# Graph convolution, first layer: each gather waits for a unit of the product, and the next layer's weights are loaded in the fourth group

## The chip, the cores and the metric

One core of a Trainium2 chip. The metric is the device time of one execution in microseconds (us); the median of ten executions of the kernel before is 502.68 us (502.14 to 503.23). Engines: PE (TensorE; its weight loads are listed as PEld), DVE (VectorE), ACT (ScalarE), POOL (GpSimd) and SP (SyncE, which here only issues DMAs).

## The reference

A layer norm and a relu, then three layers of edge convolution over 80,000 edges between 2,500 nodes of 256 features, then one product over the four concatenated stages, added to x. The edges come sorted by target.

```python
def _edge_conv(x, src, dst, W, b):
    xi = x[dst]
    xj = x[src]
    m = jnp.concatenate([xi, xj - xi], axis=-1) @ W + b
    s = jax.ops.segment_sum(m, dst, num_segments=N)
    cnt = jax.ops.segment_sum(jnp.ones((dst.shape[0],), m.dtype), dst, num_segments=N)
    return s / jnp.maximum(cnt, 1.0)[:, None]
...
for W, b in ((W0, b0), (W1, b1), (W2, b2)):
    h = jax.nn.relu(_edge_conv(h, src, dst, W, b))
    xs.append(h)
cat = jnp.concatenate(xs, axis=-1)
return cat @ Wf + bf
...
h = jnp.maximum(_layernorm(x, axis=-1), 0.0)
x = x + _L0_gnn_ref(h, edge_index, ...)
```

## The kernel before

`by_windows` turns the segment sum into a product. `a` holds, for a group of targets, how many edges go from each of 2,560 padded nodes to each target. A layer first forms z, the nodes times the lower half of W, split in two parts `zh` and `zl` whose sum is z. It then forms z times `a`, to which it adds the nodes times the upper half.

**Groups and units.** Targets 112 to 2,499 stand in five groups (`NG`) of at most 480. `layer` (L989) computes one group as a generator: 20 units of four matmuls (two halves of the features, `zh` and `zl`, for one tile of 128 nodes) and four units with the weights `wt`. In the first layer the counts of the next group are made between the units (`build`, `finish`). In the first layer, the matmuls of all five groups, 120 units, run from 61 to 198 us. The loop over the groups of the first layer (from L1079) also steps a generator `extra` once or twice a unit; it holds the small works that are to be spread out: the degrees of the nodes (`degrees`), `later_loads`, and `shares` in the last group.

**The first 112 targets** (`FEW`) aren't in the groups. For them z is gathered edge by edge: z of the first layer is stored to `z_dram[0]` (`keep_nodes`: `zh` from SP's queue, `zl` added to it from POOL's), and `gather(0)` (L918) issues 56 gathers (`EDGES`) from POOL, one for the e-th edge of every target, each of 128 rows of 1 KB. `who` gives the rows; where a target has no e-th edge it points at one fixed row of padding (`NONE`, L618). The gathers go to the eight places of `sums` in turn, from the ninth on adding to what is there. `add_sums` (L926) adds `b_all` times the degree, then adds the eight places up on DVE and splits the result in two parts; `layer_few` (L977) takes it into PSUM with two matmuls against `only` for each half of the features, after the ones with `wt`.

**Order.** An engine called through `InOrder` (PEo, DVEo, POOLo, ACTo, SPo) keeps the order in which the program was written; what is called without it is placed by a scheduler. On PE `layer_few(0)` stands after the last unit of the first layer and before `nodes_split` (L784), the first step of layer 1. In layers 1 and 2 the gathers are made by `gather_pairs` (L954), without adding, and from the fifth pair on the first of each pair waits for the latest matmul unit issued in the program.

**Loads and stores on SP.** `later_loads` (L1065) loads layer 1's weights (`wb`, `wt`, `wf`), the bias rows `b_all` of layer 0 and `bf_sb`. `store_a` writes the counts of the first four groups to DRAM when they are complete, four stores each, for layers 1 and 2.

Of the kernel before, what the change touches and what calls it, by code (L numbers as in the profile page):

```python
# [11 lines left out]
OP = mybir.AluOpType  # L12
# [295 lines left out]
def chain(*its):  # L308
    for it in its:
        yield from it  # L310
# [3 lines left out]
def by_windows(ctx: ExitStack, tc: tile.TileContext, x, src, dst, Ws, bs, Wf, bf, out, missing):  # L314
    nc = tc.nc
    PE, DVE, ACT, POOL, SP = nc.tensor, nc.vector, nc.scalar, nc.gpsimd, nc.sync
    PEo, DVEo, POOLo, ACTo, SPo = (InOrder(tc, e) for e in (PE, DVE, POOL, ACT, SP))
# [3 lines left out]
    NT = (N + P - 1) // P  # L321
# [3 lines left out]
    DC = D // P  # L325
# [7 lines left out]
    EDGES = 56  # L333
    SUMS = 8
# [3 lines left out]
    WG = (NW + P - 1) // P  # L338
# [36 lines left out]
    def bank():  # L375
        return ps[-1].tile([P, 512], F32, name="bank")
# [42 lines left out]
    def tile_of(z, t):  # L419
        return z[:, t % 2, t // 2 * D:(t // 2 + 1) * D]  # L420
# [23 lines left out]
    def load_wb(l, queue=SP):  # L444
        ws[l] = wpool.tile([P, DC, D], F32, name="wt"), wpool.tile([P, DC, D], F32, name="wb", bufs=1)
        queue.dma_start(ws[l][1], Ws[l][D:2 * D, :].rearrange("(c p) d -> p c d", p=P))

    def load_wt(l, queue=SP):
        queue.dma_start(ws[l][0], Ws[l][0:D, :].rearrange("(c p) d -> p c d", p=P))
# [205 lines left out]
    def degrees(i):  # L655

        for q in range(W + 2):
            junk = hot.tile([P, CAP], BF16, name="junk2")
            ACTo.activation(junk, away[:, i, :], AF.Relu, bias=nc_[:, q:q + 1], accum_out=gsum[:, i, q:q + 1])
            yield  # L660
        DVEo.scalar_tensor_tensor(deg[:, i, :], gsum[:, i, 1:W + 1], -2.0, gsum[:, i, 0:W], op0=OP.mult, op1=OP.add)
        DVEo.tensor_add(deg[:, i, :], deg[:, i, :], gsum[:, i, 2:W + 2])
        DVEo.tensor_copy(deg_b[:, i, :], deg[:, i, :])
        yield
        yield
        yield
        yield
        for w0 in range(0, min(P, NW - i * P), P // 2):
            n = min(P // 2, NW - i * P - w0)
            pc = bank()  # L670
            for c in range(W):
                PEo.matmul(pc[:, :n * W].rearrange("p (w c) -> p w c", c=W)[:, :, c],
                          deg_b[:, i, c:c + 1].to_broadcast([P, P]), ident_b[:, w0:w0 + n], start=True, stop=True)
            to = FEW + (i * P + w0) * W
            ACTo.copy(cnt[:, to:to + n * W], pc[:, :n * W])
            yield
        if i == WG - 1:
            pc = bank()
            PEo.matmul(pc[:, :FEW], deg_b[:, i, 0:1].to_broadcast([P, P]), ident_b[:, IN_LAST:IN_LAST + FEW],
                       start=True, stop=True)  # L680
            ACTo.copy(cnt[:, :FEW], pc[:, :FEW])
            yield
# [136 lines left out]
    def group_of(g):  # L819
        return FEW + sum(GWS[:g]) * W, GWS[g] * W  # L820
# [5 lines left out]
    def new_a(g):  # L826
        return apools[g % 2].tile([P, NT, GS], F32R, name="a")
# [50 lines left out]
    def finish(g, a):  # L878
        c0, n = group_of(g)
        if n < GS:  # L880
            DVEo.memset(a[:, :, n:].bitcast(F32), 0.0)
        ACTo.copy(a[PAD:PAD + 1, NT - 1, :n], cnt[PAD:PAD + 1, c0:c0 + n])
        if g + 1 < NG:
            store_a(g, a)
        yield

    def store_a(g, a, queue=SP):

        for t in range(0, NT, 5):
            queue.dma_start(a_dram[g][:, t:t + 5, :], a[:, t:t + 5, :].bitcast(F32))  # L890
# [13 lines left out]
    def keep_nodes(l, a, b):  # L904
# [4 lines left out]
        def tiles_of(z):  # L909
            return z[:, :, a // 2 * D:b // 2 * D].bitcast(F32).rearrange("p i (q d) -> p i q d", d=D)  # L910
# [4 lines left out]
        for i, q in ways:  # L915
            POOLo.dma_start(to[:, i, q, :], tiles_of(zl)[:, i, q, :], accum_op=OP.add)

    def gather(l):  # L918

        for e in range(EDGES):  # L920
            POOLo.indirect_dma_start(
                out=sums[:, e % SUMS, :], out_offset=None, in_=z_dram[l][:, :],
                in_offset=bass.IndirectOffsetOnAxis(ap=who[:, e:e + 1], axis=0),
                **({"compute_op": OP.add} if e >= SUMS else {}))

    def add_sums(n):  # L926

# [9 lines left out]
    def room(as_=F32):  # L937

        return hot.tile([P, BW * CH, P], BF16, name="one_m", bufs=AHEAD).rearrange(
            "p k m -> p (k m)").bitcast(as_).rearrange("p (i d) -> p i d", i=2)  # L940
# [13 lines left out]
    def gather_pairs(l):  # L954

        got = []
        for k in range(EDGES // 2 + PAIRS):
            if k >= PAIRS:
                if k == PAIRS + 1:
                    DVEo.tensor_add(sums[:, :2, :], got[0], got[1])  # L960
                elif k > PAIRS:
                    DVEo.tensor_add(sums[:, :2, :], sums[:, :2, :], got[k - PAIRS])
            if k < EDGES // 2:
                two = room()
                got.append(two)
                for i in range(2):
                    d = POOLo.indirect_dma_start(
                        out=two[:, i, :], out_offset=None, in_=z_dram[l][:, :],
                        in_offset=bass.IndirectOffsetOnAxis(ap=who[:, 2 * k + i:2 * k + i + 1], axis=0))
                    if k >= PAIRS and i == 0:  # L970

                        tc.add_manual_dep(d.ins, unit[0].ins.name, mybir.DependencyInfo(
                            mybir.DependencyClass.Sync, mybir.DependencyReason.DATA), reason="spread over the layer")
            if k >= PAIRS - 1:
                yield

# [10 lines left out]
    unit = [None]  # L987

    def layer(l, g, a, own, PE=PE, ACT=ACT):  # L989

        c0, n = group_of(g)
        pa = ps_agg.tile([P, DC, 512], F32, name="pa")
        ways = [(o, c) for o in range(DC) for c in range(DC)]
        units = [(0, k) for k in BY_TURNS]
        for i, u in enumerate(own):
            units.insert(u + i, (1, i))
        last = {}
        for kind, i in units:
            last.update({o: (kind, i, o) for o in (range(DC) if kind == 0 else ways[i][:1])})
        for kind, i in units:  # L1000
            if kind == 0:
                for o in range(DC):
                    for z in (zh, zl):
                        unit[0] = PE.matmul(pa[:, o, :n], tile_of(z, i)[:, o * P:(o + 1) * P], a[:, i, :n],  # L1004
                                            start=(i == 0 and z is zh),
                                            stop=(z is zl and last[o] == (kind, i, o)))
            else:
                o, c = ways[i]
                unit[0] = PE.matmul(pa[:, o, :n], ws[l][0][:, c, o * P:(o + 1) * P], hT[:, c, c0:c0 + n],  # L1009
                                    start=False, stop=(last[o] == (kind, i, o)))  # L1010
            yield
        ACT.activation(hT[:, :, c0:c0 + n], pa[:, :, :n], AF.Relu)  # L1012
# [8 lines left out]
    a = new_a(0)  # L1021
# [43 lines left out]
    def later_loads():  # L1065
        load_wb(1, SPo)
        load_wt(1, SPo)
        load_wf(1, SPo)
        load_b_all(0, SPo)
        SPo.dma_start(bf_sb, bass.AP(tensor=bf.tensor, offset=bf.offset, ap=[[0, P], [1, D]]))  # L1070
        yield
# [2 lines left out]

    held = None
    LATE = [NT] * 4
    gather(0)
    extra = chain(degrees(0), finish(0, a), later_loads(), degrees(1))
    for g in range(NG):  # L1079
        at = {}  # L1080
        own = LATE
        if g + 1 < NG:
            a1 = new_a(g + 1)
            one = build(g + 1, a1)
            left = -(-len([b for b in windows if b[0] == g + 1]) // TURN)
            units = NT + DC * DC
            at = {(i + 1) * (units - 1) // left - 1 for i in range(left)}
            if g:
                own = [u + 1 - i for i, u in enumerate(sorted(at)[1:5])]
        else:  # L1090
            extra = shares()
        for u, _ in enumerate(layer(0, g, a, own, PEo, ACTo)):
            if u in at:
                next(one)
            next(extra, None)
            if g == 0 and u % 2:
                next(extra, None)
            if g == 0 and u == NT // 2 + 3:
                by_count(0)
            if u == NT - 1 and g + 1 < NG:  # L1100
                run(extra)
                by_count(g + 1)
                if g == NG - 2:
                    by_count(NG)
        run(extra)
        if g + 1 < NG:
            run(finish(g + 1, a1))
            held, a = a, a1
        extra = chain(degrees(g + 2) if g + 2 < WG else ())
    layer_few(0, add_sums(SUMS))  # L1110
    DVEo.tensor_sub(ws[1][0], ws[1][0], ws[1][1])
    tiles = {NG - 1: a, NG - 2: held}
# [81 lines left out]
```

## Time and profile before

| | |
|---|---|
| median of 10 executions | 502.68 us |
| the profiled execution | 502.23 us |
| its span | 500.4 us |
| granted PE clock | 0.998 |
| first layer's last unit ends on PE | about 198.4 us |
| first gather starts | 76.34 us |
| last gather starts | 184.52 us |
| gathers of the first layer (`sums<-z_dram,who`) | 56, mean 1660 ns on POOL |
| loads of `later_loads` issued by SP | 76.12 to 80.2 us |
| stores of `a`, groups 1 to 3, issued by SP | 91.35 to 152.0 us, 12 of 1200 KB |

All times in a profile are counted from the start of the span. A line of a timeline gives the start, the length, the engine, the line of code, the operation, what it writes and reads, and in brackets how long the engine was idle before it and what ended that idle time. Operations of the ordered engines all stand under L282, the line of the helper. In the table by stretch the columns are: the stretch, its length, busy time and instructions of PE, PEld, DVE, ACT and POOL, the granted PE clock, the mean busy share of the 16 DMA engines, and GB/s. A DMA queue's line gives its packets, its MB and the time of its packets as a share of 16 engines' stretch; q0 is POOL's queue, q1 SP's. "DMA to landing" is the time from the start of the issuing instruction to the last byte's arrival.

### The profile page before, as it was taken

Reading aid. Unit: us, or ns where it says so; the run is one execution under the profiler, and the core shown is the slowest. Engines: PE = TensorE matmul, PEld = TensorE weight load, DVE = VectorE, ACT = ScalarE, POOL = GpSimd, SP = SyncE. Lnnn points to the kernel's source line nnn. Section 1 sums busy time; section 2 is a strip of 40 time slices with the busy share of each in tenths; the row PEclk is TensorE's granted clock in tenths of the full one; section 3 lists DMA queues with packets and bytes.
Section 4 is the critical chain, followed back from the end, with each engine's and each line's share of the span. In section 5 each row is a group of like instructions: output and inputs, shape, how many; then the busy total and the mean of one; then the engine's idle time right before and its main releaser. Section 6 shows DMA issues by size and latency. Waiting matters only on the chain.

```text
span 500.4 us, 7649 instructions
## 1 busy us (share of the span) xinstructions
PE 490.5 (98%) x2863; PEld 403.1 (81%) x2863; DVE 265.7 (53%) x670; ACT 135.1 (27%) x309; POOL 251.7 (50%) x234
## 2 busy tenths in 40 slices
PE   8999999999999999999999999999999999999994
PEld 4888888778788887888788787878887878778783
DVE  7999988888998802771243131427623231214043
ACT  5676577655634311510000000005200000000000
POOL 3688307888888870025777482600276545451000
PEclk9999999999999999999999999999999999999999
DMA  9416998796969994477999999963338699998032
GB/s 278 152 52 130 245 294 250 286 225 177 325 104 362 117 79 47 159 266 308 348 282 347 212 278 247 93 116 126 106 105 331 231 300 218 263 240 84 2 117 94
DMA packets 42104, 100.01 MB, mean 200 GB/s; under 512 B 5209, under 2 KB 32170, under 8 KB 36394
## 3 DMA queue, kind: packets, MB, share of 16 engines
q1 hardware_dynamic: 22762, 70.06, 38.5%
q0 software_dynamic: 18368, 28.26, 35.7%
q10 hardware_dynamic: 928, 1.11, 0.7%
q8 instruction: 24, 0.39, 0.3%
q14 instruction: 22, 0.18, 0.1%
HBM read 61.79 MB, written 38.26 MB: 200 GB/s over the span
## 4 chain that ended last, share of the span: by engine, by line
PE 91%; DVE 4%; DMA 2%; POOL 1%; SPq 0%; issue 0%; ACT 0%; DVEq 0%; ACTq 0%
PE pa L1004 34%; PE pa L282 22%; PE bank L811 10%; PE bank L282 7%; PE bank L787 7%; PE pa L1009 6%; PE pz L282 3%; DMA acc<-in_x_dram 2%; DVE one_m L282 1%; DVE st L282 1%; DVE one_n L282 1%; POOL acc L282 1%; DVE zl L282 0%; DVE away L282 0%; SPq L282 0%; PE turned L282 0%
## 5 line engine op out<-in xcount | busy, mean ns | idle before, releaser
L282 POOL DMA_INDIRECT one_m<-z_dram,who x112 | 110.6, 988 | 145.8 <-DVE acc L282 70.9
L1004 PE MATMUL pa<-a,zh 128*128 128x480 f32 (+1 forms) x400 | 151.8, 379 | 0.0
L1004 PE MATMUL pa<-a,zl 128*128 128x480 f32 (+1 forms) x400 | 151.7, 379 | 0.0
L282 POOL DMA_INDIRECT sums<-z_dram,who x56 | 93.0, 1660 | 25.4 <-issue 16.8
L282 DVE TENSOR_TENSOR sums<-sums,one_m 128x512 f32<-128x512 f32 x52 | 36.1, 693 | 105.9 <-DMA one_m<-z_dram,who 105.5
L1004 PEld LDWEIGHTS pa<-a,zl 128*128 128x128 f32 x400 | 75.0, 187 | 12.1
L1004 PEld LDWEIGHTS pa<-a,zh 128*128 128x128 f32 x400 | 75.1, 188 | 10.3
L282 PE MATMUL pa<-a,zh 128*128 128x480 f32 (+1 forms) x200 | 81.1, 406 | 0.0
L282 PE MATMUL pa<-a,zl 128*128 128x480 f32 (+1 forms) x200 | 75.7, 379 | 0.0
L282 DVE TENSOR_TENSOR one_m<-iota_m,key_m 128x1024 bf16<-128x1024 bf16 x100 | 68.6, 686 | 13.3 <-PE bank L282 12.4
L1012 ACT ACTIVATE hT<-pa 128x960 f32<-128x960 f32 (+1 forms) x10 | 9.7, 966 | 230.2 <-PE pa L1009 230.2
L282 ACT CAST a<-bank 128x480 fp32r<-128x480 f32 x100 | 50.6, 566 | 54.6 <-PE bank L282 53.5
L282 DVE TENSOR_TENSOR one_n<-iota_n,key_n 128x480 bf16<-128x480 bf16 x200 | 63.8, 359 | 0.0
L282 DVE SCALAR_TENSOR_TENSOR acc<-bank,share,acc 128x256 f32<-128x256 f32 x60 | 28.5, 482 | 55.1 <-PE bank L811 55.1
L811 PE MATMUL bank<-wf,hT 128*128 128x256 f32 x240 | 53.7, 379 | 0.5 <-ACT hT L282 0.5
L811 PEld LDWEIGHTS bank<-wf,hT 128*128 128x128 f32 x240 | 45.5, 190 | 9.8 <-issue 3.4
L282 PEld LDWEIGHTS <-one_m 128*128 128x128 bf16 x796 | 37.3, 98 | 9.0 <-issue 3.4
L282 PEld LDWEIGHTS pa<-a,zh 128*128 128x128 f32 x200 | 37.7, 188 | 8.2 <-issue 3.1
L282 PEld LDWEIGHTS pa<-a,zl 128*128 128x128 f32 x200 | 37.7, 188 | 6.9 <-issue 2.1
L282 PE MATMUL bank<-one_n,one_m 128*128 128x120 bf16 (+1 forms) x796 | 42.4, 208 | 0.1
L787 PE MATMUL bank<-wb,hT 128*128 128x256 f32 x160 | 35.0, 380 | 0.0
L1009 PE MATMUL pa<-hT,wt 128*128 128x480 f32 (+1 forms) x80 | 33.7, 564 | 0.0
(148 smaller groups left out, 418.6 us busy)
## 6 DMA issues: line engine op xcount, KB each, us to landing
a<-a_dram SPq DMA_DIRECT2D x24, 1200.0 KB, 14.0
a_dram<-a SPq DMA_DIRECT2D x20, 1200.0 KB, 14.4
out_dram<-acc SPq DMA_DIRECT2D x19, 128.0 KB, 1.7
z_dram<-one_m SPq DMA_DIRECT2D x16, 128.0 KB, 1.7
z_dram<-sums SPq DMA_DIRECT2D x16, 128.0 KB, 1.7
acc<-in_x_dram POOLq DMA_DIRECT2D x4, 512.0 KB, 12.6
z_dram<-zh SPq DMA_DIRECT2D x7, 256.0 KB, 5.1
z_dram<-zl POOLq DMA_DIRECT2D x7, 256.0 KB, 6.9
```

Of the source, the lines that this page charges most:

```text
L282: return self.tc.keep_in_program_order(call(*args, **kwargs))
L787: PE.matmul(pz[:, :D], hT[:, c, t * P:(t + 1) * P], ws[l][1][:, c, :], start=(c == 0), stop=(c == DC - 1))
L811: PE.matmul(po[:, :D], hT[:, c, t * P:(t + 1) * P], wfs[l][:, c, :], start=(c == 0), stop=(c == DC - 1))
L1004: unit[0] = PE.matmul(pa[:, o, :n], tile_of(z, i)[:, o * P:(o + 1) * P], a[:, i, :n], start=(i == 0 and z is zh), stop=(z is zl and last[o ...
L1009: unit[0] = PE.matmul(pa[:, o, :n], ws[l][0][:, c, o * P:(o + 1) * P], hT[:, c, c0:c0 + n], start=False, stop=(last[o] == (kind, i, o)))
L1012: ACT.activation(hT[:, :, c0:c0 + n], pa[:, :, :n], AF.Relu)
```

## The change

`gather` becomes a generator: each gather gets a dependency on the latest matmul unit of `layer` that has been written (`unit[0]`), and the loop over the units steps it so that the 56 gathers stand behind units 11 to 111 of the 120. `later_loads` leaves the first group's `extra` (an empty step takes its place there) and comes in the fourth group.

```diff
+    def behind_unit(d):
+
+        tc.add_manual_dep(d.ins, unit[0].ins.name, mybir.DependencyInfo(
+            mybir.DependencyClass.Sync, mybir.DependencyReason.DATA), reason="spread over the layer")
+
     def gather(l):
 
         for e in range(EDGES):
-            POOLo.indirect_dma_start(
+            behind_unit(POOLo.indirect_dma_start(
                 out=sums[:, e % SUMS, :], out_offset=None, in_=z_dram[l][:, :],
                 in_offset=bass.IndirectOffsetOnAxis(ap=who[:, e:e + 1], axis=0),
-                **({"compute_op": OP.add} if e >= SUMS else {}))
+                **({"compute_op": OP.add} if e >= SUMS else {})))
+            yield
...
-    gather(0)
-    extra = chain(degrees(0), finish(0, a), later_loads(), degrees(1))
+    FIRST, LAST_ONE = 10, 5 * (NT + DC * DC) - 8
+    edge = gather(0)
+    fetched, passed = 0, 0
+    extra = chain(degrees(0), finish(0, a), [None], degrees(1))
     for g in range(NG):
...
         for u, _ in enumerate(layer(0, g, a, own, PEo, ACTo)):
+
+            passed += 1
+            while fetched < EDGES and (passed - FIRST) * EDGES > fetched * (LAST_ONE - FIRST):
+                next(edge)
+                fetched += 1
             if u in at:
                 next(one)
...
-        extra = chain(degrees(g + 2) if g + 2 < WG else ())
+        extra = chain(degrees(g + 2) if g + 2 < WG else later_loads() if g + 2 == WG else ())
```

`NT` is 20 and `DC` is 2, so `LAST_ONE` is 112; `WG` is 4, so `later_loads` is stepped in the group with g = 3. In `gather_pairs` the same dependency is now written with `behind_unit`; nothing else changes there.

In the built program PE, DVE, ACT and POOL have the same instructions in the same order as before; every gather of the first layer has a wait for PE more. On SP the five loads, which stood before the stores of groups 1 to 3, stand behind these twelve stores.

More of the change, by code (lines that the diff above doesn't have):

```diff
@@ L970, in gather_pairs @@
                     if k >= PAIRS and i == 0:
-                        tc.add_manual_dep(d.ins, unit[0].ins.name, mybir.DependencyInfo(
-                            mybir.DependencyClass.Sync, mybir.DependencyReason.DATA), reason="spread over the layer")
+                        behind_unit(d)
             if k >= PAIRS - 1:
```

## The prediction

> **What bounds the kernel now.** I read the page first, the chain of waits next, then the timelines of the engines around 180 to 200 us, and last the gathers' times to landing by stretch. The page gives TensorE (PE) 98% of the span and 91% of the chain:
>
> ```profile
> PE 490.5 (98%) x2863; PEld 403.1 (81%) x2863; DVE 265.7 (53%) x670; ACT 135.1 (27%) x309; POOL 251.7 (50%) x234
> ...
> PE 91%; DVE 4%; DMA 2%; POOL 1%; SPq 0%; issue 0%; ACT 0%; DVEq 0%; ACTq 0%
> ```
>
> The chain between 172 and 202 us has PE pieces alone; "start, length, what":
>
> ```profile
> 178.99 20.66 PE pa L282 x96
> 199.65 2.43 PE bank L787 x11
> ```
>
> So the first layer's end is set by the product, not by the gathers. How near the gathers come is in the timelines of POOL (two last gathers), DVE (`add_sums`) and PE's weight loads (the matmul of `layer_few` that takes the sums):
>
> ```profile
> 182.67 1.54 POOL L282 DMA_INDIRECT sums<-z_dram,who  x1 [0.30 <-issue]
> 184.52 1.54 POOL L282 DMA_INDIRECT sums<-z_dram,who  x1 [0.30 <-issue]
> ```
>
> ```profile
> 194.39 2.41 DVE L282 TENSOR_TENSOR sums<-sums 128x1024 f32<-128x1024 f32 x3 [10.81 <-DMA sums<-z_dram,who]
> 196.83 0.29 DVE L282 CAST one_m<-sums 128x256 fp32r<-128x256 f32 x1
> 197.16 0.42 DVE L282 TENSOR_TENSOR one_m<-sums,one_m 128x256 fp32r<-128x256 f32 x1
> ```
>
> ```profile
> 198.54 0.30 PEld L282 LDWEIGHTS pa<-only,one_m 128*128 128x128 f32 x2
> ```
>
> The last gather starts at 184.5 and DVE waits 10.8 us for it; the sums are ready at 197.58, and PE takes them at 198.54. The slack is 0.96 us, 0.9 with the hand-over. That is all the room in which this change may delay the last gather.
>
> How long does a gather take to land? The view of the tile `sums`, for gathers started in 111 to 119 us (no store under way) and in 157 to 186:
>
> ```profile
> DMA to landing us min/median/max: 3.8/3.9/4.0
> ```
>
> ```profile
> DMA to landing us min/median/max: 9.8/11.7/13.3
> ```
>
> The shortest, 9.8, is the last one's (184.52 + 9.8 = 194.3). What lies between is a queue, and the table by stretch shows it: the DMA share is over 1 from 150 to 194, at 329 GB/s while the stores of `a` run and at only 82 GB/s after them:
>
> ```profile
> 150.00:166.00 16.00, 16.00 (x145) 12.79 (x144) 12.71 (x33) 6.75 (x14) 13.56 (x9) 1.00 1.04 329
> 166.00:194.00 28.00, 28.00 (x195) 23.81 (x194) 9.34 (x31) 5.34 (x10) 17.01 (x11) 1.00 1.07 82
> 194.00:199.00 5.00, 5.00 (x22) 3.24 (x21) 3.66 (x6) 0.59 (x1) 0.00 (x0) 1.00 0.00 0
> ```
>
> The DMA queues by stretch give the price of one gather: in 108 to 119 us, and in 167 to 190, with packets, MB and share of the 16 engines:
>
> ```profile
> q0 software_dynamic: 1024, 0.93, 59.7%
> ```
>
> ```profile
> q0 software_dynamic: 1974, 1.79, 108.3%
> ```
>
> A gather moves 128 KB (0.131 MB). Early: 0.93 MB are 7.1 gathers in 59.7% of 11 us, 0.92 us each. Late: 1.79 MB are 13.7 gathers in 23 us, 1.68 us each, and the engines are full. The late gathers cost nearly double with no store beside them; I suspect the padding of `who`, which points every missing edge at one row of z, since the later a gather the more of its rows are padding.
>
> **The change part by part.**
>
> *Nothing is gained on PE.* The PE order is the same, and from 61 to 199 us the chain holds PE pieces alone. Gathers out of DVE's way could help only where PE waits for DVE or ACT there: by the list of waits PE's weight loads wait for them some 4 us in all, in pieces of 0.2 us that mostly lie under running matmuls. Bounds 0 and -1 us; I take 0.
>
> *When the last gather is issued.* Gather e (from 0) goes out when (passed - 10) x 56 > e x 102: e = 47 behind unit 96, e = 48 behind 98, e = 55 behind 111, the 15th unit of the fifth group. That group's first unit is done before 178.99; a unit is 4 matmuls, and 80 take 16.92 us in the chain at L1004, so 0.85 us. Unit 98 ends at 180, unit 111 at 178.99 + 14 x 0.85 = 190.9. But POOL needs 1.54 + 0.30 = 1.85 us a gather (the rows above: 184.52 - 182.67), more than the 1.8 units x 0.85 = 1.55 us between the waits. So POOL sets the pace: 180.0 + 7 x 1.85 = 193.0, 8.5 us later than before.
>
> *When it lands.* From below: 193.0 + 3.9 = 196.9 by the undisturbed row. From above: 193.0 + 11.7 = 204.7 by the median of the full queue. Between them I keep accounts. From 149 to 194.3 the DMA engines were full, so added work moves the end one to one if the queue still never empties. Before, 36 gathers had been started by 145 and had landed by about 149; now the 35th and 36th come behind units 72 and 74, at 149 and 151, so two more gathers join the jam: 2 x 1.3 (between 0.92 and 1.68) = 2.6 us. The moved loads join it as well (next part): 3.4. That makes 194.3 + 6.0 = 200.3. Does the queue stay filled? The gathers from 166 to 178 come every 1.82 units of 1.2 us, 2.2 us, which drains 0.5 us a gather, some 3 us in all of a backlog that was 13.3 - 3.9 = 9 us; at 180 it still holds some 5 us, and the last eight come at 1.85 against 1.68. It stays filled.
>
> *The loads.* Before, SP issued them at 76 us; now they stand behind the twelve stores of groups 1 to 3, the last of which SP issues at 149.0 to 152.0, in the same DMA queue:
>
> ```profile
> 149.00 3.00 SPq L890 DMA_DIRECT2D a_dram<-a  x4
> ```
>
> They land when the stores have (about 166) plus a few us, so by 172. Their first users are `add_sums` (b_all, 183 at the earliest) and `nodes_split` (wb, 199.65): waits at nothing, covered by 11 us and more. Their price is DMA time inside the jam, 1.05 MB. In 149 to 166.7 SP's queue moved 4.92 MB in 69.3% of 17.7 us, 2.5 us a MB: 2.6 us from below. In 76 to 87 the loads and one store part of 1.23 MB took 66.4% of 11 us, 7.3 us; less 1.23 x 2.5 = 3.1, 4.2 us for the loads: from above. I take the middle, 3.4. On SP nothing that is due waits behind them: the next is `missing` and the b_all load of layer 1.
>
> *The wait on POOL.* Behind the gathers on POOL stands nothing until the gathers of layer 1 at 221.9, before which POOL idles 35.9 us: covered.
>
> *The wait that results.* Landing to sums ready: 197.58 - 194.3 = 3.3 us, as before; PE can bear 0.9 us. A landing at 200.3 holds PE for 200.3 - 194.3 - 0.9 = 5.1 us. Behind that matmul on PE, in order, stand `nodes_split`, the final products and all of layer 1. From 199 us on the chain is PE almost throughout, so nothing takes the delay back.
>
> The Trainium skill's "DMA: Bandwidth & Descriptors", section "Anatomy of one DMA — SWDGE (gpsimd) path", gives a DMA issued from GpSimd about 2.0 us plus its bytes over 436 GB/s, an estimate of 2.3 us for 128 KB; by it the last gather would land at 195.3 and PE would wait 0.1 us, no change at all. The trace has 3.8 us at the least and 9.8 at that very place, since the page's formula knows no queue; I go by the trace.
>
> **The sum.** The profiled execution took 502.23 us, 500.4 of it span; the median of ten is 502.68. 500.4 + 5.1 = 505.5 of span; on the median, 502.7 + 5.1 = 507.8 us. The forecast's own range: landing at 199 to 202, PE held 3.8 to 6.8, 506.5 to 509.5.
>
> **The rivals.**
>
> *The queue drains before the end.* If the spread gathers and the loads fit into time that the full engines only seem to use, the last gather lands on its own: at 196.9 with early packets, at 193.0 + 3.9 + (1.68 - 0.92) = 197.7 with late ones. PE held 1.7 to 2.5 us: 504.4 to 505.2. For it: 6.0 us of added work is an account, and a share over 1 says that packets overlap. Against it: the landings after 166, far from any store, still take 9.8 to 13 us.
>
> *The queue is as deep as before.* The last gather lands 9.8 to 11.7 us after its start, at 202.8 to 204.7: held 7.6 to 9.5, so 510.3 to 512.2. For it: the last eight come at the old pace. Against it: those of the fourth group come slower than before.
>
> *Not slower.* POOL issues as fast as its first eight gathers (1.08 + 0.30 = 1.4 us a gather, the row at 80.89), keeps up with the units and starts the last at 191.2; with 3.8 us it lands at 195.0, before the point that decides, 195.2, and PE never waits: 502.7, or 501.7 with the 1 us of relief on PE. For it: the gather is then in step with PE. Against it: an accumulating gather took 1.54 us even where nothing queued (the shortest of 111 to 119), and the queue would have to be empty.
>
> That the waits do nothing, and gathers go out as before, is excluded: gather 55 can't start before unit 111, at 190.9.
>
> **How the numbers follow.** Forecast 0.66, drained queue 0.17, deep queue 0.12, not slower 0.05. I predict 507.8. The range takes all of the forecast's own (506.5 to 509.5) and reaches into the drained and the deep queue until about a fifth is left out: 504.9 to 510.3. A measurement of this kernel tells 0.2%, 1.0 us, from no change; all but the last rival pass it: slower 0.95, within 0.03, faster 0.02.
>
> **What would show it.** Right: PE idle of some 5 us ahead of the `only` matmul of `layer_few`, ended by DVE, and DVE in turn by the last gather; that gather started near 193 and landed near 200; the loads landed between 166 and 172. Wrong: the last gather started before 191, or landed within 4 us of its start, or the five groups of layer 0 ended more than 1 us earlier or later than 198.5.

## The result, and the profile after

| | before | after |
|---|---|---|
| median | 502.50 us (501.98 to 503.47, 28 runs) | 510.96 us (510.67 to 511.48, 8 runs) |
| ratio, 95% interval | 1 | 1.0166 (1.0157 to 1.0175) |
| the profiled execution, its span | 502.23, 500.4 us | 509.97, 508.2 us |
| granted PE clock | 0.998 | 0.992 |
| last gather starts, lands | 184.52, 194.3 us | 193.17, 203.0 us |
| `nodes_split` of layer 1 ends | 216.98 us | 226.40 us |

The kernel became 8.5 us slower, 3.2 us more than forecast and 0.7 us above the range. The page of the changed kernel has the same work on PE, with 1.8 us more of busy time, and a chain that is no longer PE's alone:

```profile
PE 492.3 (97%) x2863; PEld 404.4 (80%) x2863; DVE 265.6 (52%) x670; ACT 135.2 (27%) x309; POOL 254.7 (50%) x234
...
PE 88%; DVE 5%; DMA 4%; POOL 1%; issue 0%; SPq 0%; ACT 0%; DVEq 0%; ACTq 0%
```

Its chain of waits from 186 us on ("start, length, what") shows where: where the kernel before had PE pieces alone, PE now hangs on DVE, DVE on the last gather, and the gather on POOL.

```profile
191.32 1.54 POOL sums L282
192.86 0.30 issue
193.17 9.84 DMA sums<-z_dram,who
...
203.09 1.24 DVE sums L282
...
205.88 2.20 PE pa L282 x8
208.08 18.33 PE bank L787 x80
226.40 4.32 PE bank L811 x20
```

PE's weight loads of the changed kernel, in the timeline, have the length of the wait in the brackets:

```profile
205.88 0.29 PEld L282 LDWEIGHTS pa<-only,one_m 128*128 128x128 f32 x1 [7.29 <-DVE one_m L282]
```

The `only` matmul starts 7.3 us later than before (205.88 against 198.57 on PE). That is not yet the whole loss: `nodes_split` ends 9.4 us later. The remaining 2.1 us lie in the two lines after the wait: from `only` to `nodes_split` 2.20 us where it took 1.08, and 18.33 us for the 80 matmuls of `nodes_split` that took 17.33. The table by stretch of the changed kernel says why; its eighth figure after the stretch and its length, ahead of the DMA share, is the granted PE clock:

```profile
199.00:203.00 4.00, 0.00 (x0) 0.00 (x0) 0.00 (x0) 0.32 (x1) 0.00 (x0) 1.00 0.70 84
203.00:210.00 7.00, 4.12 (x13) 3.59 (x14) 3.66 (x6) 0.42 (x2) 0.00 (x0) 0.51 0.13 37
210.00:220.00 10.00, 10.00 (x48) 8.79 (x48) 7.92 (x22) 5.62 (x12) 0.00 (x0) 1.00 0.40 134
```

From 203 to 210 us PE had half its clock: the clock fell during the wait, at 203.1, 4.4 us after PE's last matmul had ended at 198.8, and PE worked on at half speed for its first 4 us (e4 below tests that the wait is the reason). The account of the profiled executions is 7.3 + 1.1 + 1.0 = 9.4 us, and it is still 9.4 us at the last accumulation of the kernel. Behind that the one profile has 6.0 us of tail and the other 4.4, which makes 7.8 us of span; of the runs below e2 has a tail of 6.0 and all others of 4.3 or 4.4, whatever their edits, so this is not taken as an effect of the change. The 8.5 us between the medians lie between these two figures. The profiled execution of the changed kernel was 1.0 us under its median. Ratios leave out executions over 1.5% above the fastest of the same kernel, which ran at a lower granted clock, so they can differ a little from the ratio of two medians.

### The profile page after: what moved, and what is told of

It reads as the page before. It is cut to its first block, busy times and chain, and to the rows that moved or that the text cites. A ratio compares the mean times of both kernels' runs of the same rounds, so it can differ in the third digit from the quotient of the medians.

```text
span 508.2 us, 7704 instructions
## 1 busy us (share of the span) xinstructions
PE 492.3 (97%) x2863; PEld 404.4 (80%) x2863; DVE 265.6 (52%) x670; ACT 135.2 (27%) x309; POOL 254.7 (50%) x234
## 4 chain that ended last, share of the span: by engine, by line
PE 88%; DVE 5%; DMA 4%; POOL 1%; issue 0%; SPq 0%; ACT 0%; DVEq 0%; ACTq 0%
PE pa L1008 34%; PE pa L282 20%; PE bank L811 10%; PE bank L282 7%; PE bank L787 7%; PE pa L1013 6%; PE pz L282 3%; DMA sums<-z_dram,who 2%; DMA acc<-in_x_dram 2%; DVE one_m L282 1%; DVE st L282 1%; DVE one_n L282 1%; POOL acc L282 1%; DVE zl L282 0%; DVE sums L282 0%
## 5 line engine op out<-in xcount | busy, mean ns | idle before, releaser
L282 POOL DMA_INDIRECT one_m<-z_dram,who x112 | 109.4, 977 | 147.8 <-DVE acc L282 72.0
L282 POOL DMA_INDIRECT sums<-z_dram,who x56 | 97.1, 1734 | 28.2 <-PE pa L282 16.4
L787 PEld LDWEIGHTS bank<-wb,hT 128*128 128x128 f32 x160 | 31.1, 195 | 4.3
```

The costliest lines, as they stand in the source:

```text
L282: return self.tc.keep_in_program_order(call(*args, **kwargs))
L787: PE.matmul(pz[:, :D], hT[:, c, t * P:(t + 1) * P], ws[l][1][:, c, :], start=(c == 0), stop=(c == DC - 1))
```

## The experiments

The first four ran on one chip, with 502.39 us (502.03 to 502.73, 19 runs) for the kernel before. On the two chips of the later runs the kernel before itself took 504.6 to 514.5 us; the changed kernel, run again on one of these (f3), took 510.92 us as on the first. So the later runs are held against these 510.92 us, and their ratios to the kernel before only stand beside them. For e5 to e12 that is a comparison between chips; f1 and f2 ran beside f3.

### Which of the two parts: e1_loads_late and e2_spread_only

One has the loads alone moved, the other the gathers alone spread:

```diff
 # e1_loads_late, against the kernel before
-    extra = chain(degrees(0), finish(0, a), later_loads(), degrees(1))
+    extra = chain(degrees(0), finish(0, a), [None], degrees(1))
...
-        extra = chain(degrees(g + 2) if g + 2 < WG else ())
+        extra = chain(degrees(g + 2) if g + 2 < WG else later_loads() if g + 2 == WG else ())
```

```diff
 # e2_spread_only, against the changed kernel
-    extra = chain(degrees(0), finish(0, a), [None], degrees(1))
+    extra = chain(degrees(0), finish(0, a), later_loads(), degrees(1))
...
-        extra = chain(degrees(g + 2) if g + 2 < WG else later_loads() if g + 2 == WG else ())
+        extra = chain(degrees(g + 2) if g + 2 < WG else ())
```

> The loads alone are moved; the gathers go out as before. If the moved loads take DMA time from the gathers in the full queue (theory): some 4 us, the last gather lands near 198.3 instead of 194.3, PE waits 2.6 us (194.3 plus the slack of 1.4) and loses up to 1 us more at a lower clock: 505 to 506 us. If the loads cost nothing there and the spreading does all (rival): 502.5. If the loads do all (second rival): 511.

> The gathers alone are spread; the loads stay in the first group. Theory: four more gathers in the jam than before, no loads: the last lands near 199 to 200, PE waits 3.3 to 4.3 us and loses some 1 us at a lower clock: 506.5 to 508. If the loads cost nothing (rival): 511. If the loads do all (second rival): 502.5 to 503.

Measured: loads alone 502.36 us, ratio 1.0015 (1.0001 to 1.0029); spreading alone 509.92 us, 1.0155 (1.0138 to 1.0172). DVE's timeline, first of e1, then of e2, has the addition that takes the last gather:

```profile
195.76 2.41 DVE L282 TENSOR_TENSOR sums<-sums 128x1024 f32<-128x1024 f32 x3 [10.25 <-DMA sums<-z_dram,who]
```

```profile
200.29 2.41 DVE L282 TENSOR_TENSOR sums<-sums 128x1024 f32<-128x1024 f32 x3 [9.51 <-DMA sums<-z_dram,who]
```

Before, this stood at 194.39. The loads alone put it off by 1.4 us, which the slack all but swallows: PE takes the sums at 198.64, and `nodes_split` starts 0.4 us later than before. So e1's theory (505 to 506) was a miss. Four of its ten executions took 504.1 to 504.3 us, though, the other six 500.8 to 502.5; the profiled one is the shortest, so what the longer ones lost is not shown.

Spreading alone puts the addition off by 5.9 us and has `only` start at 203.09 in place of 198.57, with PE idle for 4.0 us of that. The clock fell as well (0.52 from 202 to 209 us), `nodes_split` took 19.26 us, and the time is above the theory's 506.5 to 508. With both parts together the addition starts at 203.09, so by these two profiles the loads cost another 2.8 us of landing behind spread gathers, though only 1.0 us of the median (510.96 - 509.92). So nearly all of the loss is the spreading. The landing of kernels with the same gathers and loads differs, however: 201.5 in e4, 202.0 in f3, 202.3 in e3, 203.0 here.

Why 5.9? A gather's time to landing in the changed kernel, for the two gathers started at 141.40 and 143.46 and then for the one at 146.02 (the view of the tile `sums`):

```profile
DMA to landing us min/median/max: 4.3/4.4/4.5
```

```profile
DMA to landing us min/median/max: 9.6/9.6/9.6
```

So what starts by 144 us lands freely, and what starts at 146 is in the jam behind the stores. POOL's timeline of the kernel before and of the changed one around that point:

```profile
144.93 1.67 POOL L282 DMA_INDIRECT sums<-z_dram,who  x1 [0.31 <-issue]
146.90 2.54 POOL L282 DMA_INDIRECT sums<-z_dram,who  x1 [0.30 <-issue]
```

```profile
143.46 1.90 POOL L282 DMA_INDIRECT sums<-z_dram,who  x1 [0.30 <-PE bank L282]
146.02 3.36 POOL L282 DMA_INDIRECT sums<-z_dram,who  x1 [0.65 <-PE pa L282]
```

Before, the gather at 144.93 is the 36th, the last to go free; after, the one at 143.46 is the 32nd. Four gathers more are in the jam, and 5.9 / 4 is 1.5 us each, between the two prices of the prediction (0.92 and 1.68). This is an account, not yet a test; e7 below takes the four gathers out of the jam again.

### What the wait costs: e3_few_later and e4_fillers

e3 keeps the change, late landing and all, and puts `layer_few(0)` behind the first eight `nodes_split` of layer 1. e4 keeps PE busy during the wait with 32 matmuls whose result nobody reads.

```diff
 # e3_few_later, against the changed kernel
-    layer_few(0, add_sums(SUMS))
-    DVEo.tensor_sub(ws[1][0], ws[1][0], ws[1][1])
...
-        for t, zf in zip([t for t in range(1, NT) if t not in last] + last + [0], rooms(l)):
+        for j, (t, zf) in enumerate(zip([t for t in range(1, NT) if t not in last] + last + [0], rooms(l))):
+            if l == 1 and j == 2 * AHEAD:
+                layer_few(0, add_sums(SUMS))
+                DVEo.tensor_sub(ws[1][0], ws[1][0], ws[1][1])
             nodes_split(l, t, zf)
```

```diff
 # e4_fillers, against the changed kernel, in layer_few
+            if l == 0 and o == 0:
+                spare = bank()
+                for _ in range(32):
+                    PEo.matmul(spare, ident_b, cnt[:, :512], start=True, stop=True)
             for i in range(2):
                 PEo.matmul(pa[:, o, :FEW], two[:, i, o * P:(o + 1) * P], only, start=False, stop=(i == 1))
```

> The changed kernel with layer_few moved behind the first eight products of nodes_split, so that PE has about 7 us and more of work before it needs the sums. If PE's wait at layer_few is the whole loss (theory): no wait is left, no lower clock follows, 502.5 to 503.2, though the last gather lands as late as in the changed kernel. If the late gathers or loads slow something else too (rival): 504 and more.

> The changed kernel with 32 matmuls of no use on PE ahead of the two that take the sums (7 us of the 7.3 us wait). The landing is not earlier. If the 2.1 us that the matmuls after the wait lost came from a clock that falls while PE is idle (theory): 508.9. If they were slow for another reason, such as DMA traffic or the order (rival): 511.

e3 took 501.60 us (501.33 to 502.05), ratio 0.9983 (0.9973 to 0.9992), a little under its theory: the whole loss is gone, though the last gather still lands late, at 202.3. PE's wait for the sums has shrunk to this, and the clock stays whole:

```profile
210.54 0.19 PEld L282 LDWEIGHTS pa<-only,one_m 128*128 128x128 f32 x1 [1.08 <-DVE one_m L282]
```

So the gathers may be late and the engines may be full; what costs is that PE's order asks for the sums at 198.6. This is also the fastest version on this chip, 0.17% under the kernel before, about as little as can be told.

e4 took 507.28 us (507.18 to 507.45), ratio 1.0097 (1.008 to 1.0114). Its table by stretch has no fall of the clock:

```profile
203.00:210.00 7.00, 7.00 (x38) 5.27 (x37) 4.00 (x10) 1.78 (x4) 0.00 (x0) 1.00 0.23 71
```

Between the profiled executions (509.97 and 507.45) 2.5 us are gained. `only` starts 0.5 us earlier (205.38), the way from there to `nodes_split` takes 1.2 us in place of 2.2, and `nodes_split` 17.32 in place of 18.33: 0.5 + 1.0 + 1.0. So 2.0 us are the clock's, as in the account above. The 0.5 is not the fillers' doing: in this run the last gather landed 1.5 us earlier, so that DVE had the first half of the split at 204.35, and PE was still at the fillers. Adding useless work to PE made the kernel faster. The medians differ by 3.7 us; the 1.2 us above the 2.5 come from where the two profiled executions stand to their medians.

The Trainium skill's "TensorE: Matmul & The Clock Gate", section "What's actually happening", has the rate of PE halve after about 3.4 us without work, and come back after as long a stretch of work; the section "HAM oscillation — how this bites in real kernels" warns of gaps longer than that. The fall here came 4.4 us after PE's last matmul, and 3.2 us after it in e2, so near that figure; e9 below has one after an idle of only 2.1 us. In both runs here it lasted 6.8 us, some of which PE was still waiting.

### Why the late gathers are slow: e5_real_rows and e6_sixteen_rows

The prediction suspected the padding of `who`. e5 leaves the masking of `who` out, so that every gather reads rows of real edges and the sums of the first 112 targets are no longer the reference's; e6 keeps the masking and spreads the padding over 16 rows of zeros in place of one.

```diff
 # e5_real_rows, against the changed kernel
-        POOLo.tensor_scalar(who, es[:, :EDGES], -NONE, None, op0=OP.add)
+        POOLo.tensor_scalar(who, es[:, :EDGES], 0, None, op0=OP.add)
         POOLo.tensor_scalar(own, away[:, WG - 1, :EDGES], 1.0, None, op0=OP.is_equal)
-        POOLo.tensor_tensor(who, who, own, op=OP.mult)
-        POOLo.tensor_scalar(who, who, NONE, None, op0=OP.add)
```

```diff
 # e6_sixteen_rows, against the changed kernel
-        POOLo.tensor_scalar(who, es[:, :EDGES], -NONE, None, op0=OP.add)
+        none = pp.tile([P, EDGES], I32, name="none")
+        POOLo.iota(none, pattern=[[1, EDGES]], base=0, channel_multiplier=1)
+        DVEo.tensor_scalar(none, none, 15, None, op0=OP.bitwise_and)
+        POOLo.tensor_scalar(none, none, NONE - 15, None, op0=OP.add)
+        POOLo.tensor_tensor(who, es[:, :EDGES], none, op=OP.subtract)
         POOLo.tensor_scalar(own, away[:, WG - 1, :EDGES], 1.0, None, op0=OP.is_equal)
         POOLo.tensor_tensor(who, who, own, op=OP.mult)
-        POOLo.tensor_scalar(who, who, NONE, None, op0=OP.add)
+        POOLo.tensor_tensor(who, who, none, op=OP.add)
```

> The changed kernel with who pointing at the row of the next edge in the list instead of the one row of padding (leaves out the masking, so the first 112 targets' sums are over 56 edges each). If the late gathers are slow because most of their rows are one and the same (theory): the late packets fall from 199 to about 102 ns, a late gather takes 0.7 to 0.9 us of the engines instead of 1.68, the queue drains by 185 us, the last gather lands about 4 us after its start, near 197.3, PE waits some 1.5 us, perhaps without a fall of the clock: 503.5 to 505.5. If they are slow because many adding gathers are in flight (rival): landing near 202 as before, 510.5 to 511.

> The changed kernel with the padding spread over 16 rows of zeros, by (target + edge) modulo 16, which is computed with three more instructions on POOL and DVE ahead of the first layer. Theory: as with the real rows, 503.5 to 505.5, if 16 neighbouring rows are enough to take the jam apart; if neighbouring rows share what makes them slow: between that and 511. Rival (many adding gathers in flight): 510.5 to 511.

e5 took 504.05 us (503.50 to 504.57), e6 504.15 us (502.49 to 504.48): 6.9 and 6.8 us under the changed kernel's 510.92. Their ratios to the kernel before on that chip are 0.9863 (0.9813 to 0.9912) and 0.986 (0.9807 to 0.9912). The DMA queue of POOL from 178 to 196 us, with packets, MB and share of the 16 engines, first in the changed kernel, then in e5 and e6:

```profile
q0 software_dynamic: 1453, 1.32, 106.5%
```

```profile
q0 software_dynamic: 1335, 1.22, 49.4%
```

```profile
q0 software_dynamic: 1312, 1.20, 47.0%
```

Nearly the same bytes take half the engine time: 106.5% of 18 us for 1.32 MB is 1.90 us for a gather of 0.131 MB; in e5 and e6 the same working gives 0.95 and 0.92 us, the price of an early gather. But this share is not what holds the gathers up. e3 (above) and e11 (below) have the one padding row, and from 178 to 196 us they show

```profile
q0 software_dynamic: 1521, 1.38, 58.6%
```

```profile
q0 software_dynamic: 1524, 1.38, 50.2%
```

with landings as late as ever: the last gather took 8.4 us in e3 and 10.5 in e11. Why the share differs so among kernels with one padding row is not shown. The pace tells them apart. While gathers are queued, from 168 to 174 us, POOL's queue moves, in the changed kernel and then in e6,

```profile
q0 software_dynamic: 419, 0.38, 65.3%
```

```profile
q0 software_dynamic: 799, 0.73, 76.5%
```

So gathers with one padding row come through at 2.1 us each there (1.7 to 1.8 from 178 to 196 us), those with sixteen at 1.1, with SP's queue moving no less beside them. In this stretch the ten profiles with one padding row have 0.30 to 0.48 MB on POOL's queue, the eight with sixteen or with real rows 0.67 to 0.91. The slow landings of the late stretch are thus the padding: many reads of one row. With it gone the jam drains in time, as the chain of e6 shows:

```profile
193.52 3.82 DMA sums<-z_dram,who
```

The gather lands 3.8 us after its start, as on an empty queue (3.9 in e5), and PE waits little:

```profile
200.21 0.19 PEld L282 LDWEIGHTS pa<-only,one_m 128*128 128x128 f32 x1 [1.27 <-DVE one_m L282]
```

The waits of 1.3 to 1.4 us in e6 and e5 did not touch the clock: it is 1.000 and 0.999 over the profiled executions of e5 and e6, and `nodes_split` takes 17.3 us in both. The drained queue of the prediction's first rival is thus what the kernel would have had without the one padding row.

### Starting earlier: e7_earlier, e8_rows_and_later

```diff
 # e7_earlier, against the changed kernel
-    FIRST, LAST_ONE = 10, 5 * (NT + DC * DC) - 8
+    FIRST, LAST_ONE = 10, 5 * (NT + DC * DC) - 24
```

e8 is e6 with the edit of e3.

> The changed kernel with LAST_ONE 16 units earlier: the gathers stand behind units 11 to 95, so that about 37 have been started when the stores of the fourth group begin, as in the kernel before, and the last starts near 184. If the loss comes from when the gathers go out (theory): the last lands at 195 to 197.5 with the moved loads, PE waits 0 to 1.8 us: 502 to 504.5. If the waits on PE themselves slow POOL or PE (rival): 507 and more.

> The sixteen padding rows together with layer_few behind the first eight products of nodes_split: a version that might beat both. Theory: the sums are ready before PE comes to them, PE never waits, 501.5 to 502.5; nothing is to be won beyond that, because PE has no idle time left there. Rival (something beside the wait at layer_few is slower): 504 and more.

e7 took 503.84 us (502.17 to 508.89), ratio 0.9914 (0.9863 to 0.9966); e8 503.04 us (502.21 to 503.32), 0.9841 (0.9791 to 0.9891). In e7 the last gather's line in the chain is

```profile
185.08 11.13 DMA sums<-z_dram,who
```

so it starts about where it did before, is slow as before, and lands at 196.2, with 0.6 us or less of waiting on PE. Its 36th gather starts at 145.09, as in the kernel before, so no more gathers than there are in the jam, and the landing is 0.5 us from e1's 195.7, which has the same loads and the early gathers. That supports the count of four. The profiled execution took 503.00 us at a whole clock; four of the ten took 505.6 to 508.9 at a clock of 0.991 to 0.995, and what they lost has no trace. e8, with neither cause left, missed its 501.5 to 502.5 and is no better than e3 alone was on the first chip: both have 0.7 us of PE idle where DVE comes to the sums in its order, and what else e8 loses is not shown.

### Do the cures add, and do they carry over: e9 to e12

e9 is the kernel before with the sixteen rows of e6; e10 and e11 repeat e6 and e7; e12 has the sixteen rows and `LAST_ONE` less 16 in place of 8.

> The kernel before, with the padding spread over sixteen rows and nothing else. Theory: the jam after 166 us is gone, the last gather lands 4 us after its start, near 188.5 instead of 194.3; PE did not wait before either, so on a chip where the kernel before takes 502.5 the time stays there (502 to 503), and on one where the kernel before takes 505 to 514 it comes back to about 502.5 to 503.5, if there PE waits for late gathers. Rival (the longer times of that chip have another cause): they stay.

> The changed kernel with sixteen rows of padding, as in e6, once more beside another run of the kernel before. Theory: the last gather lands at 197.3, PE waits 1.6 us, no fall of the clock: 503.8 to 504.5, 0.2 to 0.4% over the kernel before where that is at 502.5. Rival: 502.5 or less, if the difference in e6 was the chip's.

> The gathers behind units 11 to 95 with the one row of padding and the late loads, as in e7, once more. Theory: the last lands near 196, PE waits 0.5 to 1 us: 502.5 to 504 where the kernel before takes 502.5.

> Sixteen rows of padding and the gathers behind units 11 to 103: both causes of the late landing taken away, the gathers still spread and the loads still late. Theory: the last gather starts near 188 and lands near 192, PE never waits: 502 to 503, the same as the kernel before, since nothing else was to be gained. If it is below 502 by more than the interval, the spreading does gain something that the wait hid (rival).

| | median (range) | ratio to before, 95% |
|---|---|---|
| e9_rows_before | 508.94 (505.89 to 515.64) | 0.9996 (0.9951 to 1.004) |
| e10_sixteen_again | 504.00 (503.73 to 504.40) | 0.9899 (0.9826 to 0.9972) |
| e11_earlier_again | 505.02 (502.62 to 507.18) | 0.9915 (0.9876 to 0.9953) |
| e12_rows_and_earlier | 502.76 (501.57 to 504.00) | 0.9873 (0.9818 to 0.9928) |

e12 has both cures, no wait at `layer_few`, and the lowest median of this chip. e10 came where its theory had it; e11 is longer than its 502.5 to 504. e9 was a miss. Its gathers are fast and done early, and yet it is long, so the jam at the end is not what makes the kernel before long on this chip. Its chain has PE idle once, with no releaser that the profile shows:

```profile
90.56 0.88 PE pa L282 x2
91.44 2.14 issue
93.58 4.41 PE pa L282 x12
```

and its table by stretch a half clock after that, which lasts 3.4 us:

```profile
93.60:97.20 3.60, 3.60 (x10) 3.02 (x11) 1.26 (x4) 2.44 (x6) 2.99 (x3) 0.53 0.98 360
```

In e12 the chain loses 0.6 us near this place (87.7 to 88.3), ended by ACT's making of `a`, and the clock stays whole; e10 and e11 have no idle of PE there.

### The changed kernel on the other chips: f1 to f4

Four kernels side by side on a third chip: f1 is e12, f2 is e6, f3 the changed kernel itself, f4 is e1.

> Sixteen rows of padding and the gathers behind units 11 to 103, as in e12. Where the kernel before takes 502.5: 502 to 503 if nothing but PE's wait is at stake (theory). Where it takes 505 to 514, as in the two calls before this: 502 to 504, if the spread gathers spare PE the idle time of unknown cause that was seen there at 91 us.

> Sixteen rows of padding in the changed kernel, as in e6 and e10. Theory: 503.8 to 504.5 wherever it runs, from a landing at 197.3 and a PE wait of 1.0 to 1.6 us.

> The changed kernel itself. Theory: 510.5 to 511.5 wherever it runs, since its wait is in its own order; where the kernel before takes 505 to 514 the two may then look alike. Rival: it is longer by 8.5 us than the kernel before on every chip.

> The loads alone late, as in e1. Where the kernel before takes 502.5: 502 to 503. Where it takes 505 to 514: as much as that if the early burst of gathers is at fault there, 502 to 504 if the early loads are.

| | median (range) | ratio to before, 95% |
|---|---|---|
| f1_rows_and_earlier | 502.55 (501.89 to 503.79) | 0.9866 (0.9814 to 0.9918) |
| f2_sixteen | 504.32 (502.80 to 504.79) | 0.9895 (0.9826 to 0.9964) |
| f3_changed | 510.92 (510.39 to 514.48) | 1.0035 (0.9999 to 1.0072) |
| f4_loads_late | 507.24 (503.29 to 509.40) | 0.9923 (0.988 to 0.9965) |

The changed kernel takes the same time here as on the first chip, by the same way: its last gather lands at 202.0, `only` waits 6.1 us, the clock is 0.55 from 203 to 210. The equal time is partly chance: this landing is 1.0 us earlier than on the first chip, and PE idles 1.7 us at 385 us, with no releaser in the profile, which the first chip's profile does not have. f1, f2 and f3 came where their theories had them. Against it the sixteen rows save 6.6 us and the earlier gathers with them 8.4, in the same runs. f1's chain is PE's alone again:

```profile
185.90 14.76 PE pa L282 x69
200.66 17.33 PE bank L791 x80
217.99 4.32 PE bank L815 x20
```

What differs on this chip is the kernel before: 511.05 us (504.68 to 513.3, 23 runs), so that the change costs next to nothing against it. f4, whose gathers are as early as before's, lies between its two forecasts (four executions at 503.3 to 503.8, six at 507.2 to 509.4). Its profile has PE idle for 2.8 us in pieces between 85 and 91 us and half a clock for 3.4 us after. Of the profiled kernels with spread gathers on these chips, e12 and f1 have 0.9 us of idle there and the others none, and in none does the clock fall there. So on these chips the spreading seems to take an early loss away and brings a late one; on the first chip the early loss is not there. This is argued, not shown: no profile of the kernel before was taken on these chips, and what makes PE idle there stays open.

## Why the prediction was wrong

**The direction and the mechanism held.** The wait appeared at the place named, PE's `only` matmul, ended by DVE, which the last gather ended; nothing took the delay back, and e3 shows that the whole loss hangs on this wait. *The PE order gains nothing*: right on the first chip, where layer 0's product ends at 198.8 as before.

**When the last gather is issued: right.** 193.0 was forecast by POOL's pace of 1.85 us; it started at 193.17, 1.85 us behind the one before it.

**The step that failed** is "two more gathers join the jam: 2 x 1.3 (between 0.92 and 1.68) = 2.6 us". It counted the kernel before at 145 us and the changed one at 149, where units 72 and 74 would have issued the 35th and 36th. At one and the same moment, 144 to 146 us, 36 had gone out before and 32 after. Four more gathers joined, for 5.9 us (e2), 3.3 us more than the sum had. In e7, where they do not join, the landing is 196.2.

**Terms that were mis-sized.** The loads were 3.4 us in the sum; they cost 1.4 us of landing alone (e1) and 2.8 behind the spread gathers by the profiles of e2 and of the changed kernel, 1.3 to 2.8 with the other landings above. The landing was thus 194.3 + 5.9 + 2.8 = 203.0 in place of 200.3. The loads landed later than the 166 to 172 forecast, `wf` at 178.2 and `bf_sb` at 182.1, and no engine waited for them. The slack was 1.4 us, not 0.9: the first `only` matmul needs the first half of the split alone, done at 197.12, while the prediction waited for the second, done at 197.58. From the true landing the wait is 203.0 - 194.3 - 1.4 = 7.3, as measured.

**A term that was missing.** The price of a wait was taken as its length. The clock's fall added 2.1 us (2.0 by e4; in e2 3.0, namely 1.1 and 1.9 us in the same two lines). A wait of 5.1 us, as forecast, would most likely have had this too: e2's start of `only` was 4.5 us late. All in all 5.1 + 3.3 - 0.6 (loads) - 0.5 (slack) + 2.1 (clock) is the 9.4 us of the profiles; between the medians it is 8.5.

**The rivals.** The deep queue gave numbers near those that came: landing 202.8 to 204.7, held 7.6 to 9.5, 510.3 to 512.2; the last gather landed at 203.0, 9.8 us after its start, and the time is 510.96. That is partly luck: 2.1 us of the time are the clock's, which that rival did not have, the wait was 7.3, and e2, e3, e4 and f3 had their last gather land after 6.8, 8.4, 8.3 and 8.6 us. The drained queue failed because of the padding row, as e6 shows: its last gather landed at 197.3, within that rival's 196.9 to 197.7, and its 504.15 us are 0.3 below the rival's 504.4 to 505.2. That suspicion was in the prediction, and was used only to price a gather; it was not asked whether it decides the queue. The prediction also read a share over 1 as the sign of the full queue; e3 and e11 have the same late landings at half of it.

## What to carry to other kernels

Work that a later stage needs is spread with its landing in mind, not its issue: here the loss went when the last piece started 8 us earlier (e7, most of it), when its reader stood eight steps later (e3), or when the padding was spread over sixteen rows (e6, most of it). When pieces are delayed past a jam, count at one moment how many have gone in each version. And the waits of 4 and 7 us on PE cost more than their length, since the half clock comes on top; useless matmuls in the gap bought that part back. Where a queue is suspected, compare times to landing and bytes per us before the share of the engines.

## What the runs showed of the hardware

Gathers that read one DRAM row many times come through slowly when they are queued: 1.7 to 1.8 us for 128 KB with one padding row from 178 to 196 us (1.32 MB in 18 us in the changed kernel, 1.38 in e3 and e11), where sixteen padding rows let the queue drain and the last gather land after 3.8 us. The time of a packet does not show this reliably: with one padding row it was 211 ns in the changed kernel (106.5% of 18 us x 16 engines / 1453), 111 in e3 and 95 in e11, with real rows 107 and with sixteen padding rows 103. The Trainium skill's "DMA: Bandwidth & Descriptors", section "Anatomy of one DMA — SWDGE (gpsimd) path", goes by the bytes alone, which makes an estimated 2.3 us of such a gather; the adding gather took 3.8 us even with the queue empty (e6).

A PE idle of 2.1 us was followed by half a clock of 3.4 us in e9, while the waits of 1.3 to 1.4 us in e5 and e6 and an idle of 1.7 us in f3 had none. In the 3.4 us before each fall (as long as the half clock lasted in e9 and f4) PE was busy for 0.0 us in the changed kernel, 0.2 in e2, 1.3 in e9 and 1.4 in f4; around the idles that had no fall it was busy for 1.7 or more of any 3.4 us. So the fall seems to go by how little PE worked, and not by one unbroken gap; no run tests this. And the same kernel before took 502.4 us on one chip and 510 to 512 on two others; the idle of PE around 85 to 93 us that goes with early gathers there has for the most part no releaser in the profile, and stays open.
